# Nine taps in other partitions of a 16-row group, and the first layer's weights in one run per partition

## The chip, the core and the metric

The kernel runs on one core of one Trainium2 chip. The metric is the time of one execution on the device in microseconds (us).

## What is computed

The input `x` has 16 images of 256 channels and 28 x 28 points. It goes through a group normalisation and then through a residual block of two layers, in which each 3 x 3 convolution is replaced by a soft lookup: for every channel the nine values around a point (a patch) are compared with 16 centroids, the softmax over the 16 distances is taken, and it weighs rows of a table made from the centroids and sub-weights. The reference, cut to this:

```python
def amm_conv3x3(x, centroids, w_sub, stride=1):
    B = x.shape[0]
    C, k, s = centroids.shape            # 256, 16, 9
    patches = jax.lax.conv_general_dilated_patches(x, (3, 3), (stride, stride), 'SAME')
    p = patches.reshape(B, C, s, Ho * Wo).transpose(0, 3, 1, 2)
    d = jnp.sum(p * p, axis=-1)[..., None] - 2.0 * jnp.einsum('bncs,cks->bnck', p, centroids) \
        + jnp.sum(centroids * centroids, axis=-1)[None, None]
    attn = jax.nn.softmax(-d, axis=-1)
    lut = jnp.einsum('cks,cso->cko', centroids, w_sub)
    out = jnp.einsum('bnck,cko->bno', attn, lut)
    ...
out = amm_conv3x3(gn(x), centroids1, wsub1)
out = jax.nn.relu(bn_inference(out, bn1_gamma, bn1_beta, bn1_mean, bn1_var))
out = amm_conv3x3(out, centroids2, wsub2)
out = bn_inference(out, bn2_gamma, bn2_beta, bn2_mean, bn2_var)
out = se_layer(out, se_w1, se_b1, se_w2, se_b2)
return x + jax.nn.relu(out + gn(x))
```

## The kernel before

The work is cut into 128 blocks: for each of two layers and 16 images there are four blocks, each one half of the channels (`hh`, 128 of 256) and one half of the rows (`t`, 14 of 28). All is in float32.

**Patches.** The image, normalised and padded to 30 x 30, is written from SBUF to a tensor in HBM, `home1` (layer 1, `to_home1`, L361, with the two halves of image 0's first channel half in two pieces) or `home2` (layer 2, by indirect transfers from POOL, L590). It is written twice for each channel, the second copy one element later, so that two neighbouring taps of one row of the 3 x 3 window are two rows of `home`. The function `patches` (L368 and L372) loads one set into `pt`, a tile of 128 partitions x 8 channel groups x 420. Its 128 partitions are eight groups of 16 rows. Each row of a group is one tap of one channel, or is unused. A set is six transfers: for each line `dy` of the window a large one into 16 partitions (the taps `dx` = 0 and 1, from the two copies) and a small one into 8 partitions (the tap `dx` = 2). Each partition receives eight runs of 418 elements. There are two `pt` tiles, used in turn, and two sets to a block, so 256 sets. A set is issued when PE has finished with the tile that it overwrites. In sets 1 to 4 the small transfers are issued by POOL, in all others by SP.

`tap_row(s)` says into which of the 16 rows tap `s` goes; it is used where the weights for the comparison are laid out on the host and where those of layer 2 are put together on the chip (`prep_wd0`, nine small transfers, far ahead of their use). Row 11 (`BIAS_ROW`) carries a constant. Unused rows hold ones in `pt` and zeros in the weights.

**The rest of a block.** `logits` (L384) multiplies `pt` by the centroids in 32 x 32 tiles; ACT takes the exponential (`exps`, L395); `num_b` and `num_a` (L448, L434) turn it into weighted sums and denominators; DVE takes the reciprocal and spreads it (L476, L491); DVE and POOL scale (`scale_a` L510, `scale_q` L499). `product` (L518) multiplies the results by 128 x 128 weights, seven times for the four blocks of an image in the manner of Strassen, for which POOL forms differences (`mix`, L527) and accumulators are added.

**Weights of the products.** Seven tiles `w_A11` to `w_S4`, of 128 partitions x 9 x 128. For the first layer `load_w` (L194) loads four of them from the input `in_ws1`, of 128 x 18 x 256: nine runs of 128 elements (512 B) for each partition, 1024 B apart. The others are sums and differences of these.

**Order.** It is written out by hand. `at(step, sub, f, ...)` files a call under a step and a place in it; all calls are then made in that order, so that each engine's queue is fixed. Block `j` starts at step `2 j`. The lines that place what the change touches:

```python
at(g + p - NPT, 1.5, patches, u, p, nc.gpsimd if 0 < g + p < 5 else None)
at(1, 1.65, load_w, 0, "A11")
at(3, 1.65, load_w, 0, "S3")
at(3, 1.65, load_w, 0, "A22")
at(6, 0.6, load_w, 0, "A12")
```

SP issues nearly all direct transfers, in this order.

Of the kernel before, what the change touches and what calls it, by code (L numbers as in the profile page):

```python
# [17 lines left out]
P = 128  # L18
# [6 lines left out]
PTW = RT * PW  # L25
K = 16
S = 9
NS = 9
# [26 lines left out]
def digits(h):  # L55
    g, j = h & 7, h >> 3
    return g >> 1, g & 1, j >> 2, j & 3


def tap_row(s):  # L60
    dy, dx = divmod(s, 3)
    return dy + (0, 8, 3)[dx]


BIAS_ROW = 11
# [2 lines left out]
def rows_of(m, c, a):  # L68
    r, c4, mm = c >> 1, 2 * (c & 1) + a, m & 3
    return r, c4, mm, 16 * r + 4 * mm + c4, 16 * (1 - r) + 4 * mm + c4  # L70
# [3 lines left out]
def kernel(  # L74
# [50 lines left out]
    def view(t, off, dims):  # L125
        return bass.AP(t.tensor, t.offset + off, [list(d) for d in dims])
# [62 lines left out]
    def load_w(l, n, eng=None):  # L189
        hh, o = SLOTS[n]  # L190
        t = wl[n]
        eng = eng or nc.sync
        if l == 0:
            eng.dma_start(t, ws1[:, NS * hh : NS * hh + NS, o * P : (o + 1) * P])  # L194
        else:
            eng.dma_start(t[:, 0:8, :], view(d_wa, hh * 8 * P * C + o * P, [[C, P], [P * C, 8], [1, P]]))
            eng.dma_start(t[:, 8, :], d_wb[hh * P : hh * P + P, o * P : (o + 1) * P])
# [165 lines left out]
    def patches(u, p, single=None):  # L363
        hm = (home1 if u["l"] == 0 else home2)[u["b"]]
        at0 = ((u["hh"] * P + 8 * 8 * p) * 2) * HROW + RT * u["t"] * PW
        pt = u["pt", p]
        for dy in range(3):
            nc.sync.dma_start(  # L368
                pt[dy::8, :, : PTW - 2],
                view(hm, at0 + dy * PW, [[HROW, 16], [16 * HROW, 8], [1, PTW - 2]]),  # L370
            )
            (single or nc.sync).dma_start(  # L372
                pt[3 + dy :: 16, :, : PTW - 2],
                view(hm, at0 + dy * PW + 2, [[2 * HROW, 8], [16 * HROW, 8], [1, PTW - 2]]),
            )

# [334 lines left out]
    def prep_wd0():  # L711
        st = stage()
        nc.gpsimd.memset(st[:, :512], 0.0)
        for s in range(S):
            nc.sync.dma_start(
                st[tap_row(s) :: 16, :512].rearrange("p (a k) -> p a k", k=K),
                view(d_sk, s * K, [[S * K, 8], [8 * S * K, 32], [1, K]]),
            )
# [195 lines left out]
    for j, u in enumerate(blocks):  # L914
# [3 lines left out]
        for p in range(2):  # L918
            u["pt", p] = pts[p]
            at(g + p - NPT, 1.5, patches, u, p, nc.gpsimd if 0 < g + p < 5 else None)  # L920
            for q in range(2):
                mm = 2 * p + q
                at(g + p, 0.1 + q, logits, u, mm)
                if wide and mm == 0:
                    at(g, 0.12, wide_copy, u, mm)
                    at(g, 0.9, wide_turn, u, mm)
                    at(g, 1.38, wide_max, u, mm)
                    at(g, 1.39, wide_sub, u, mm)
                    at(g + 1, 1.22, wide_back, u, mm)
                    at(g + 1, 1.89, wide_exp, u, mm)  # L930
                else:
                    at(g + p, 0.12 + q, exps, u, mm)
# [18 lines left out]
    for l in range(2):  # L951
        for b in range(B):
            n = l * B + b
# [48 lines left out]
            else:  # L1002
# [16 lines left out]
                if b == B - 1:  # L1019
                    at(g + 11, 1.9, flags)  # L1020
                    at(g + 12, 2.9, flag_sum)
# [5 lines that stand above are left out]
    for c, sub, m in ((5, 1.96, "S1"), (7, 1.96, "S3"), (7, 2.65, "S2"), (8, 1.96, "S4")):  # L1027
# [80 lines left out]
    with tc.If(rv > 0):  # L1108
        with tc.For_i(0, B, 1) as it:
            t = io.tile([P, NB, HW], F32, tag="xt", name="xt")  # L1110
# [13 lines left out]
            for l in range(2):  # L1124
# [6 lines left out]
                for t2 in range(2):  # L1131
                    us = []
                    for hh in range(2):
                        u = {"l": l, "b": B, "t": t2, "hh": hh, "w": 0, "step": None}
                        for k in range(5):
                            u["qi", k] = hh if k == 4 else 4 * hh + k
                        us.append(u)
                        for mm in range(4):
                            if mm % 2 == 0:
                                u["pt", mm // 2] = pts[mm // 2]  # L1140
                                patches(u, mm // 2)
                            logits(u, mm)
                            wide_copy(u, mm)
                            wide_turn(u, mm)
                            wide_max(u, mm)
                            wide_sub(u, mm)
                            wide_back(u, mm)
                            wide_exp(u, mm)
                        num_b(u)
                        split_r(u)  # L1150
                        join_r(u)
                        split_q(u)
                        join_q(u)
                        recip_dve(u)
                        spread(u, 4)
                        scale_q(u, 4)
                        for mm in range(4):
                            spread(u, mm)
                            num_a(u, mm)
                            scale_a(u, mm)  # L1160
# [23 lines left out]
def _lay_out(inputs):  # L1184

    import numpy as np

    f = lambda n: np.asarray(inputs[n], dtype=np.float32)
    x = f("x")
    bsz, ch = x.shape[:2]  # L1190
    arrays = {"in_x": x.reshape(bsz, ch, -1)}
    cent, wsub = f(_NAMES[0] + "1"), f(_NAMES[1] + "1")
    wd = np.zeros((P, 8, 4, 32), np.float32)
    cwa = np.zeros((P, 8, 4, 32), np.float32)
    cwb = np.zeros((P, 8, 4, 32), np.float32)
    ws = np.zeros((P, NST, ch), np.float32)
    ids = np.zeros((ch, MAPC), np.uint32)
    konst = np.zeros((P, 304), np.float32)
    before = np.zeros((P, 2, ch), np.float32)
    for c0 in range(ch):  # L1200
        i, a, m, c = digits(c0)
        r, c4, mm, rn, rs = rows_of(m, c, a)
        hh = m >> 2
        ka = slice(32 * c + 16 * a, 32 * c + 16 * a + 16)
        for s in range(S):
            wd[32 * i + 16 * a + tap_row(s), m, c, 16 * a : 16 * a + 16] = cent[c0][:, s]
        cwa[ka, m, i, 8 * c4 : 8 * c4 + 8] = cent[c0][:, :8]
        cwb[ka, m, i, rn] = cent[c0][:, 8]
        cwb[ka, m, i, rs] = 1.0
        ws[32 * i + 8 * c4 : 32 * i + 8 * c4 + 8, NS * hh + 2 * mm + r] = wsub[c0, :8]  # L1210
        ws[32 * i + rn, NS * hh + 8] = wsub[c0, 8]
        konst[ka, 3 + c4] = 1.0
        konst[ka, 48 + 32 * mm + rn] = 1.0
        konst[ka, 176 + 32 * mm + rs] = 1.0
        wa = (2 * m + r) * 16 + 4 * i + c4
        ids[c0] = (c0, (2 * c + a) * 32 + 4 * m + i, 2 * wa, 2 * wa + 1, hh * P + 32 * i + rn, 2 * c0, 2 * c0 + 1)
    nhalf = np.zeros((P, P), np.float32)
    for p in range(P):
        konst[p, 0] = p % 32 < 16
        konst[p, 1] = p % 32 >= 16  # L1220
        konst[p, 7 + (p // 16) % 2] = 1.0
        for b in range(2):
            before[p, b, : b * P + p] = 1.0
        nhalf[p, p - p % 16 + BIAS_ROW] = -0.5
        if p % 16 == BIAS_ROW:
            a = (p // 16) % 2
            konst[p, 16 + 16 * a : 32 + 16 * a] = SHIFT / 2
    arrays["in_wd1"] = wd.reshape(P, -1)
    arrays["in_cwa1"] = cwa.reshape(P, -1)
    arrays["in_cwb1"] = cwb.reshape(P, -1)  # L1230
    arrays["in_ws1"] = ws
    cent, wsub = f(_NAMES[0] + "2"), f(_NAMES[1] + "2")
    arrays["in_sk2"] = cent.transpose(0, 2, 1).reshape(ch, -1)
    arrays["in_ks2"] = cent.reshape(ch, -1)
    arrays["in_wsub2"] = wsub.reshape(ch, -1)
    arrays["in_konst"] = konst
    arrays["in_nhalf"] = nhalf
    arrays["in_before"] = before.reshape(P, -1)
    arrays["in_ids"] = ids
    names = [f"L0_conv_bn{l}_{v}" for l in "12" for v in ("gamma", "beta", "mean", "var")] + ["L0_conv_se_b2"]  # L1240
    arrays["in_vec"] = np.stack([f(n).reshape(-1, P).T for n in names], axis=2)
    for n in ("se_w1", "se_b1", "se_w2"):
        arrays["in_" + n] = f("L0_conv_" + n)
    return {n: np.ascontiguousarray(a) for n, a in arrays.items()}, x.shape
# [17 lines left out]
```

## Time and profile before

| | |
|---|---|
| median of 3 runs | 2680.17 us (2678.79 to 2683.46) |
| the profiled execution | 2684.49 us, of which its span is 2683.0 |
| mean granted PE clock in it | 0.993 |
| PE busy / DVE / ACT / POOL | 97% / 66% / 50% / 71% |
| bytes moved by DMA | 374.39 MB, mean 140 GB/s |
| DMA queue of SP (hardware) | 216008 packets, 334.87 MB, 54.0% of 16 engines' span |
| DMA queue of POOL (software) | 6944 packets, 33.95 MB, 3.5% |

The profile is of one execution. PE is the matrix engine, PEld its weight loads, DVE, ACT and POOL the vector, scalar and general engines, SPq the queue of the engine that issues transfers. A row of the timeline gives start, duration, engine, line, operation, output and inputs, and in brackets how long the engine had been idle and what ended that. An `x64` on an `L384` row means 64 matmuls; each float32 matmul of the program stands twice.

### The profile page before, as it was taken

The page shows a single profiled execution, that of the slowest core. Times are in us where ns is not written, and L with a number is a line of the kernel's source. Part 1 is how long each engine was busy: PE and PEld are TensorE (multiplying, and loading weights), DVE is VectorE, ACT ScalarE, POOL GpSimd, SP SyncE. Part 2 cuts the span into 40 slices and gives each one's busy share as a digit, 9 for nine tenths or more (in the row PEclk, how much of TensorE's full clock was granted, in tenths as well). Part 3 has the DMA queues.
Part 4 walks back from the last instruction along what each step waited for, and adds up shares of the span by engine and source line. Part 5 has one row for each costly group of instructions (what it writes and reads, how often), then busy time and mean ns, then how long its engine had stood idle before and what let it go on. Part 6 is the DMA issues. An engine that isn't in the chain of part 4 may idle for free.

```text
span 2683.0 us, 85705 instructions
## 1 busy us (share of the span) xinstructions
PE 2613.8 (97%) x36984; PEld 1261.1 (47%) x36984; DVE 1773.8 (66%) x3786; ACT 1354.7 (50%) x1873; POOL 1903.7 (71%) x1334
## 2 busy tenths in 40 slices
PE   4999999999999999999999999999999999999997
PEld 1344444444444444444444444444444444444444
DVE  4785666667666556656577767677767677767675
ACT  2443444444445444444455555555555655555653
POOL 3755677666776666766578687788787788787786
PEclk8999999999999999999999999999999999999999
DMA  8665667755666666666584555545555555555551
GB/s 180 162 158 147 155 159 201 195 139 138 158 165 168 178 156 145 164 176 158 127 191 108 111 127 123 116 111 109 122 127 123 116 113 108 121 127 123 116 114 51
DMA packets 223337, 374.39 MB, mean 140 GB/s; under 512 B 30360, under 2 KB 193736, under 8 KB 222952
## 3 DMA queue, kind: packets, MB, share of 16 engines
q1 hardware_dynamic: 216008, 334.87, 54.0%
q0 software_dynamic: 6944, 33.95, 3.5%
q8 instruction: 295, 4.83, 0.8%
q14 instruction: 90, 0.74, 0.1%
HBM read 288.93 MB, written 79.80 MB: 137 GB/s over the span
## 4 chain that ended last, share of the span: by engine, by line
PE 86%; DMA 1%; POOL 1%; issue 1%; DVE 1%; ACT 0%; SPq 0%; POOLq 0%; DVEq 0%; ACTq 0%
PE acc L518 46%; PE lg L384 15%; PE na L434 12%; PE nb L448 12%; DMA home<-hpad,col 1%; POOL qp L527 1%; PE sep L814 0%; ACT e L395 0%; DMA pt<-home 0%; PE sep L803 0%; DVE qp L510 0%; DVE rb L491 0%; POOL home L590 0%; POOL qo L525 0%; PE sqp L288 0%
## 5 line engine op out<-in xcount | busy, mean ns | idle before, releaser
L395 ACT ACTIVATE e<-lg 128x784 f32<-128x784 f32 x960 | 738.8, 821 | 720.2 <-PE lg L384 714.9
L527 POOL TENSOR_TENSOR qp<-qp,qp 128x784 f32<-128x784 f32 x512 | 944.6, 1870 | 163.5 <-DVE qp L510 163.0
L518 PE MATMUL acc<-qp,w_S 128*128 128x392 f32 x2048 | 743.2, 503 | 7.7 <-POOL qp L527 6.3
L491 DVE STREAM_SHUFFLE rb<-r 128x392 f32<-128x392 f32 x1024 | 550.6, 604 | 0.0
L518 PE MATMUL acc<-qp,w_A 128*128 128x392 f32 x1536 | 546.5, 499 | 0.1
L518 PEld LDWEIGHTS acc<-qp,w_S 128*128 128x128 f32 x2048 | 376.1, 190 | 356.6 <-POOL qp L527 39.1
L384 PE MATMUL lg<-pt,wd 32*32 32x392 f32 x16384 | 500.6, 504 | 27.0 <-DMA pt<-home 16.3
L518 PEld LDWEIGHTS acc<-qp,w_A 128*128 128x128 f32 x1536 | 284.1, 190 | 247.9 <-DVE qp L510 37.6
L510 DVE TENSOR_TENSOR qp<-na,rb 128x784 f32<-128x784 f32 x352 | 334.1, 972 | 98.1 <-PE na L434 84.9
L462 DVE SCALAR_TENSOR_TENSOR r<-nb,kst,r 128x392 f32<-128x392 f32 x128 | 79.9, 624 | 464.5 <-ACT r L458 464.5
L448 PE MATMUL nb<-e,cwb 64*32 64x392 f32 x8192 | 382.4, 497 | 2.1 <-issue 1.0
L434 PE MATMUL na<-e,cwa 64*32 64x392 f32 x8192 | 377.5, 494 | 0.1
L476 DVE RECIPROCAL r<-r 128x392 f32<-128x392 f32 x128 | 333.2, 2603 | 4.4
L499 POOL TENSOR_TENSOR qp<-qp,rb 128x784 f32<-128x784 f32 x160 | 297.4, 1871 | 2.4
L448 PEld LDWEIGHTS nb<-e,cwb 64*32 64x32 f32 x8192 | 181.4, 107 | 195.8 <-issue 57.1
L384 PEld LDWEIGHTS lg<-pt,wd 32*32 32x32 f32 x16384 | 127.5, 103 | 309.0 <-issue 261.6
L499 POOL TENSOR_TENSOR qo<-qo,rb 128x392 f32<-128x392 f32 x128 | 132.0, 1031 | 197.7 <-DVE rb L487 197.5
L434 PEld LDWEIGHTS na<-e,cwa 64*32 64x32 f32 x8192 | 182.5, 106 | 186.8 <-issue 78.0
L590 POOL DMA_INDIRECT home<-hpad,col x60 | 60.6, 1011 | 185.9 <-DMA home<-hpad,col 91.2
L458 ACT ACTIVATE r<-nb,kst 128x392 f32<-128x392 f32 x128 | 86.8, 678 | 177.4 <-PE nb L448 177.4
L419 POOL TENSOR_TENSOR z<-z,mx 128x1568 f32<-128x1568 f32 x32 | 92.1, 2879 | 86.4 <-DVE mx L413 86.4
L504 ACT COPY qp<-na 128x784 f32<-128x784 f32 x160 | 130.1, 813 | 26.0 <-PE na L434 24.0
(154 smaller groups left out, 1744.5 us busy)
## 6 DMA issues: line engine op xcount, KB each, us to landing
pt<-home SPq DMA_DIRECT2D x768, 209.0 KB
pt<-home SPq DMA_DIRECT2D x756, 104.5 KB
home<-xpad SPq DMA_DIRECT2D x31, 899.0 KB
xt<-in_x SPq DMA_DIRECT2D x30, 784.0 KB
out_dram<-y SPq DMA_DIRECT2D x32, 392.0 KB
w_S<-d_wS SPq DMA_DIRECT2D x4, 576.0 KB
st<-in_wsub SPq DMA_DIRECT2D x4, 512.0 KB
st<-d_wa SPq DMA_DIRECT2D x16, 128.0 KB
```

What stands on the lines that cost most here:

```text
L384: nc.tensor.matmul(bk[32 * c : 32 * c + 32, :N].rearrange("p (r w) -> p r w", w=W), lhsT=wts["wd", u["hh"]][32 * i : 32 * i + 32, mm, c, : ...
L395: nc.scalar.activation(eg[:, 2 * i : 2 * i + 2, :], bk[:, :, :N], AF.Exp, scale=2.0)
L419: nc.gpsimd.tensor_tensor(zk, zk, mx.unsqueeze(2).to_broadcast([P, N // 4, K]), ALU.subtract)
L434: nc.tensor.matmul(bs[32 * i : 32 * i + 32, r, :N], lhsT=wts["cwa", u["hh"]][64 * r : 64 * r + 64, mm, i, :], rhs=es[64 * r : 64 * r + 64, ...
L448: nc.tensor.matmul(bs[32 * i : 32 * i + 32, r, :N], lhsT=wts["cwb", u["hh"]][64 * r : 64 * r + 64, mm, i, :], rhs=es[64 * r : 64 * r + 64, ...
L476: nc.vector.reciprocal(u["r"], u["r"])
L491: nc.vector.stream_shuffle(rb[:, r, :], u["r"], mask_of(2 * mm + r))
L499: nc.gpsimd.tensor_tensor(q, q, u.pop(("rb", mm)), ALU.mult)
L504: nc.scalar.copy(pair(u, mm), u.pop(("na", mm))[:, :, :N])
L510: nc.vector.tensor_mul(pair(u, mm), u.pop(("na", mm))[:, :, :N], rb)
L518: nc.tensor.matmul(accs[key][:, :N], lhsT=wl[w][:, k, :], rhs=us["q", k], start=first and n == 0, stop=last and n == len(ks) - 1,)
L527: nc.gpsimd.tensor_tensor(pair(out_u, mm), pair(in0, mm), pair(in1, mm), ALU.subtract)
```

## The change

The taps of the window go to other rows of the 16-row group. Before, tap (`dy`, `dx`) went to row `dy`, `8 + dy` or `3 + dy` for `dx` = 0, 1, 2. After it a table gives the rows: 0, 8, 5 for `dy` = 0, then 4, 12, 13, then 1, 9, 2. The transfers of a set write to partitions with the same strides (8 for the large one, 16 for the small one) from other starts. Row 11 stays free for the constant.

The input `in_ws1` is laid out on the host as four blocks of 128 rows, each row the 9 x 128 elements of one partition, so that `load_w` reads one run of 4608 B for each partition.

No other instruction is added, removed or moved, on any engine.

```diff
+TAPS = ((0, 8, 5), (4, 12, 13), (1, 9, 2))
+
+
 def tap_row(s):
-    dy, dx = divmod(s, 3)
-    return dy + (0, 8, 3)[dx]
+    return TAPS[s // 3][s % 3]
...
         if l == 0:
-            eng.dma_start(t, ws1[:, NS * hh : NS * hh + NS, o * P : (o + 1) * P])
+            eng.dma_start(t.rearrange("p s n -> p (s n)"), ws1[(2 * hh + o) * P : (2 * hh + o + 1) * P, :])
...
         for dy in range(3):
             nc.sync.dma_start(
-                pt[dy::8, :, : PTW - 2],
+                pt[TAPS[dy][0] :: 8, :, : PTW - 2],
                 view(hm, at0 + dy * PW, [[HROW, 16], [16 * HROW, 8], [1, PTW - 2]]),
             )
             (single or nc.sync).dma_start(
-                pt[3 + dy :: 16, :, : PTW - 2],
+                pt[TAPS[dy][2] :: 16, :, : PTW - 2],
                 view(hm, at0 + dy * PW + 2, [[2 * HROW, 8], [16 * HROW, 8], [1, PTW - 2]]),
             )
...
-    arrays["in_ws1"] = ws
+    arrays["in_ws1"] = ws.reshape(P, 2, NS, 2, ch // 2).transpose(1, 3, 0, 2, 4).reshape(4 * P, -1)
```

## The prediction

> **What bounds the kernel now.** I read the page first: busy time, then the chain that ended last.
>
> ```profile
> span 2683.0 us, 85705 instructions
> PE 2613.8 (97%) x36984; PEld 1261.1 (47%) x36984; DVE 1773.8 (66%) x3786; ACT 1354.7 (50%) x1873; POOL 1903.7 (71%) x1334
> PE 86%; DMA 1%; POOL 1%; issue 1%; DVE 1%; ACT 0%; SPq 0%; POOLq 0%; DVEq 0%; ACTq 0%
> ```
>
> PE runs for 2613.8 of 2683.0 us. All its idle time together is 69.2 us, 2.6% of the span, and nothing that only moves data can win more than this plus what a lowered PE clock costs. So the question is how much of the 69.2 us waits for the two transfers that the diff touches. The view of PE's own waits answers it, first over the whole span (columns: total us, times, longest), then in parts.
>
> ```profile
> PE lg L384 <- DMA pt<-home: 16.3, 4, 8.0
> PE gnp L322 <- DVE gn_mv L317: 13.4, 3, 5.7
> ...
> PE lg L384 <- DMA pt<-home: 11.7, 2, 8.0
> ...
> PE lg L384 <- DMA pt<-home: 3.8, 1, 3.8
> ...
> PE lg L384 <- DMA pt<-home: 0.8, 1, 0.8
> ...
> PE acc L518 <- DMA pt<-home: 0.5, 1, 0.5
> ```
>
> The last four rows are from 0 to 60, 60 to 130, 245 to 600, and 1350 to the end: nearly all of the 16.3 us of waiting for patches lies in the first 104 us, in three waits. The timeline of PE shows them, with the issues on SP's queue that lead to each.
>
> ```profile
> 16.39 0.57 SPq L368 DMA_DIRECT2D pt<-home  x1
> 26.19 4.09 PE L384 MATMUL lg<-pt,wd 32*32 32x392 f32 x64 [8.04 <-DMA pt<-home]
> ...
> 30.38 7.92 SPq L368 DMA_DIRECT2D pt<-home  x6
> 39.94 1.62 PE L384 MATMUL lg<-pt,wd 32*32 32x392 f32 x32 [3.63 <-DMA pt<-home]
> 41.49 5.02 PE L448 MATMUL nb<-e,cwb 64*32 64x392 f32 x64
> ...
> 92.42 0.59 SPq L368 DMA_DIRECT2D pt<-home  x1
> 103.33 1.64 PE L384 MATMUL lg<-pt,wd 32*32 32x392 f32 x32 [3.76 <-DMA pt<-home]
> 104.90 4.03 PE L448 MATMUL nb<-e,cwb 64*32 64x392 f32 x64
> ```
>
> I call these sets A (8.04 us waited), B (3.63) and C (3.76): 15.4 us, all that this change can reach directly. After the fill a set is hidden:
>
> ```profile
> 2003.59 0.54 SPq L368 DMA_DIRECT2D pt<-home  x1
> 2006.60 0.58 SPq L372 DMA_DIRECT2D pt<-home  x1
> ...
> 2020.46 0.94 PE L384 MATMUL lg<-pt,wd 32*32 32x392 f32 x32
> 2005.00:2007.00 2.00, 2.00 (x7) 1.14 (x6) 2.00 (x2) 0.00 (x0) 2.00 (x2) 1.00 0.86 207
> 2009.00:2011.00 2.00, 2.00 (x47) 0.79 (x53) 1.21 (x3) 0.97 (x4) 2.00 (x2) 1.00 0.45 115
> 2011.00:2013.00 2.00, 2.00 (x61) 1.23 (x48) 0.70 (x1) 1.26 (x2) 2.00 (x2) 1.00 0.03 8
> ```
>
> (The last three are windows: length, busy time of PE, PEld, DVE, ACT, POOL, granted clock, DMA share, GB/s.) The set issued from 2003.59 has stopped moving by about 2010.5, since 115 GB/s falls to 8. It is read at 2020.46, so about 10 us of cover is left. If that cover were lost, each further microsecond would be paid in each of 256 sets; nothing in this change comes near 10 us.
>
> **The change, part by part.**
>
> **1. The taps in other rows.** A set is six transfers before and after, in the same order on the same queues (in sets 1 to 4 the three small ones go out on POOL), with the same bytes and run lengths. The issues on SP stay as they are. PE's matmuls read all 32 rows of a block whatever lies in them, so L384 keeps its duration. The weights, the bias row and layer 2's nine small transfers that place weights by tap follow the rows and do not change in number; those nine run some 70 steps before their weights are loaded and cost nothing. What can change is only how fast the six pieces are written, and that matters in A, B and C. The rows for the size and rate:
>
> ```profile
> pt<-home SPq DMA_DIRECT2D x768, 209.0 KB
> pt<-home SPq DMA_DIRECT2D x756, 104.5 KB
> 8.00:10.00 2.00, 0.24 (x1) 0.24 (x2) 1.71 (x2) 0.00 (x0) 1.92 (x2) 1.00 1.06 408
> 14.00:16.00 2.00, 0.00 (x0) 0.00 (x0) 1.93 (x5) 0.00 (x0) 0.00 (x0) 1.00 0.97 207
> 82.00:84.00 2.00, 2.00 (x56) 0.92 (x48) 1.21 (x1) 2.00 (x3) 1.96 (x2) 1.00 0.94 216
> ```
>
> At a DMA share near 1, loads over all 128 partitions move 408 GB/s (8 to 10 us), the half write of the padded image, out of 64 partitions, moves 207 (14 to 16), and patches alone move 216 (82 to 84). Equally busy queues move half as much where a transfer reaches only some of the partitions. So where the pieces go does seem to matter. But the large pieces go to every 8th partition before (rows 0/8, 1/9, 2/10) and after (0/8, 4/12, 1/9): a different start, the same stride, the same 16 partitions apart by 8. One alone should be as slow as before. They go out 1.2 us apart (3.6 us for six), and a large piece of 214,000 bytes takes 214/216 = 1.0 us at the patch rate. Hence neighbouring pieces overlap only in part, and a better spread over the whole set has little to act on.
>
> Bounds for one exposed set. Gain: before, rows 0 to 3 of a 16-row group take four of the nine taps, after it three in any four adjacent rows that start at a multiple of four (3, 2, 2, 2). If such fours were what limits a set, it would take 3/4 of the time: data flow for about 5.5 us (2005 to 2010.5), so 1.4 us sooner. Loss: the small piece to row 5 goes out just ahead of the large one to rows 4/12, the one to row 13 just behind it, in the same fours; if such neighbours slow each other by one large piece's time, a set lands 1.0 us later. I take 0 for each of A, B and C, nearest to the row of one set alone, whose stride stays. Ends: 3 x -1.4 = -4.2 and 3 x +1.0 = +3.0 us.
>
> **2. The weights of the first layer.** Four loads (the second kind of name, `w_S`, is the one at 62.14; a third `w_A` follows it at once), each now one run of 4608 B per partition in place of nine of 512 B:
>
> ```profile
> w_A<-in_ws SPq DMA_DIRECT2D x3, 576.0 KB
> 38.34 1.47 SPq L194 DMA_DIRECT2D w_A<-in_ws  x1
> 62.14 0.45 SPq L194 DMA_DIRECT2D w_S<-in_ws  x1
> 83.91 1.95 SPq L361 DMA_DIRECT2D home<-xpad  x2
> 85.92 1.11 SPq L194 DMA_DIRECT2D w_A<-in_ws  x1
> 85.00:90.00 5.00, 3.57 (x40) 1.35 (x8) 4.43 (x8) 2.61 (x4) 5.00 (x3) 1.00 1.05 333
> 90.00:95.00 5.00, 4.23 (x46) 1.66 (x50) 2.27 (x9) 0.49 (x1) 4.35 (x5) 1.00 0.89 273
> ```
>
> The first three stand before no wait of PE on a DMA: the next such wait after 39.94 is C. The fourth is ahead of C in SP's queue, behind two writes of the padded image (two of 899 KB, 1841 kB). These and the load's 590 kB are 2431 kB; 333 GB/s for 5 us is 1665 kB, and the rest at 273 GB/s takes 2.8 us, so the load ends near 92.8, while C's first piece is only issued at 92.42, after the writes have landed. It is almost out of the way already: I take 0, with -1.1 us as the far end (half of 590 kB at 273 GB/s) and no loss, since the bytes stay.
>
> **3. The clock behind a wait.** After B and C the same work runs slower: L448 takes 5.02 and 4.03 us. Undisturbed rows:
>
> ```profile
> 81.80 2.86 PE L448 MATMUL nb<-e,cwb 64*32 64x392 f32 x64
> 86.81 1.58 PE L518 MATMUL acc<-qp,w_S 128*128 128x392 f32 x4 [1.21 <-POOL qp L527]
> 40.00:42.00 2.00, 2.00 (x40) 0.49 (x48) 0.00 (x0) 0.40 (x1) 0.14 (x1) 0.50 1.09 188
> 88.00:90.00 2.00, 1.78 (x6) 0.68 (x4) 2.00 (x6) 0.00 (x0) 2.00 (x2) 1.00 1.06 374
> ```
>
> Behind the wait of 3.63 us the granted clock is 0.50; behind one of 1.21 it is 1.00. The price is (5.02 - 2.86) + (4.03 - 2.86) for L448 and (1.62 - 0.94) + (1.64 - 0.94) for the L384 before it: 4.7 us. With waits unchanged it is paid as before: 0. If B and C shrink enough it goes too.
>
> [...]
>
> Sum: 0 + 0 + 0, between -4.2 - 1.1 - 4.7 = -10.0 and +3.0. The profiled execution took 2684.49 us (1.5 beyond its span), 4.3 more than the median of 2680.17; the three runs behind the median lie 4.7 apart (2678.79 to 2683.46), so the sum is carried over as it is. A shift of the start moves all that follows by the same amount, PE having no slack behind it. Forecast: 2680 us.
>
> **The rivals.**
>
> *Faster: the spread shortens the sets.* A, B and C land 1.4 us sooner, leaving waits of 6.6, 2.2 and 2.4 us. If 2.2 to 2.4 us is below what lowers the clock, 4.2 + 4.7 = 8.9 us go: 2671.3. If not, 4.2: 2676. For it: patches move at half the rate of 128-partition loads, and the old rows leave 12 to 15 empty. Against it: the stride of 8 stays and the pieces go out 1.2 us apart.
>
> [...]
>
> *Slower: neighbouring pieces collide.* Two pairs in each set (row 5 with rows 4/12, then row 13 with these) are in flight together; at 1.0 us a pair A, B and C land 2.0 us later each, 6 us: 2686.2. It decides only where a set has no cover, and from 10 us later in the steady part. For it: the large pieces already run at half rate. Against it: the old order also sent row 3 between 0/8 and 1/9.
>
> *The change does not act at all* is my forecast in its plainest form, and gives 2680.
>
> **How the numbers follow.** A measurement of this kernel tells about 0.2%, 5.4 us, from no change. Chances: forecast 0.43; sets sooner, clock not relieved (2676) 0.16; sets sooner and clock relieved (2671.3) 0.29; slower rival 0.12. So faster by over 5.4 us 0.29, within 0.59, slower 0.12. The range from 2670 to 2685 holds the first three and leaves out the slower rival; the forecast and the 2676 case alone would span 2675 to 2683, the upper end being +3.0.
>
> **What would show it.** Right: waits of L384 on patches near 8.0, 3.6 and 3.8 us, clock 0.50 behind two of them, PE idle near 69 us, DMA share in the steady windows as before. Faster rival: GB/s well over 216 in windows of patches alone, the waits at 39.94 and 103.33 under 2.5 us, L448 at 2.9 behind them. Slower rival: A's wait over 9 us, fewer than 200 GB/s. The forecast is wrong if PE's idle time moves by over 5 us, above all if it does so after 130 us, where I found nothing that waits for these transfers.

## The result, and the profile after

The changed kernel takes 2672.56 us (median of 8 runs, 2669.08 to 2676.3), the kernel before 2678.88 us (median of 8 runs, 2675.07 to 2683.46). The ratio is 0.9976, with a 95% interval of 0.9965 to 0.9986: 6.3 us or 0.24% faster. The forecast was 2680 within 2670 to 2685. The time lies in the range, but "no change" was wrong, and so was the reason for it.

The page of the kernel after: span, busy times, SP's queue, and the chain that ended last (by engine, then by line). Line numbers are two higher than before.

```profile
span 2671.9 us, 85705 instructions
PE 2606.3 (98%) x36984; PEld 1260.6 (47%) x36984; DVE 1773.1 (66%) x3786; ACT 1353.6 (51%) x1873; POOL 1902.5 (71%) x1334
q1 hardware_dynamic: 211912, 334.87, 51.2%
PE 85%; POOL 2%; DMA 2%; issue 1%; DVE 0%; ACT 0%; SPq 0%; POOLq 0%; ACTq 0%; DVEq 0%
PE acc L520 45%; PE lg L386 15%; PE na L436 12%; PE nb L450 12%; POOL qp L529 2%; DMA home<-hpad,col 2%; POOL qo L527 0%; POOL home L592 0%; ACT e L397 0%; PE sep L816 0%; PE sep L805 0%; DVE qp L512 0%; DMA pt<-home 0%; PE sqp L290 0%; DVE y L857 0%
```

Bytes are the same (334.87 MB), but the queue's transfers keep the 16 DMA engines busy for 51.2% of the span in place of 54.0%. PE's idle time fell by only 3.6 us (69.2 to 65.6); its busy time fell by 7.5 (2613.8 to 2606.3), although it does the same work. So the time that is counted as busy can hold waiting too.

The three exposed sets after, in the timeline of PE:

```profile
26.21 4.09 PE L386 MATMUL lg<-pt,wd 32*32 32x392 f32 x64 [8.10 <-DMA pt<-home]
...
39.09 1.62 PE L386 MATMUL lg<-pt,wd 32*32 32x392 f32 x32 [2.23 <-DMA pt<-home]
40.64 4.99 PE L450 MATMUL nb<-e,cwb 64*32 64x392 f32 x64
...
102.52 1.74 PE L386 MATMUL lg<-pt,wd 32*32 32x392 f32 x32 [3.87 <-DMA pt<-home]
...
1407.82 0.82 PE L520 MATMUL acc<-qp,w_S 128*128 128x392 f32 x2
...
2659.54 0.26 PE L805 MATMUL sep<-ysum,w_sb 128*32 128x1 f32 x4 [1.05 <-DVE fi L887]
```

The last two rows have these partners before, near the end of layer 1 and at the end of the kernel:

```profile
1418.89 0.93 PE L518 MATMUL acc<-qp,w_S 128*128 128x392 f32 x2 [0.54 <-DMA pt<-home]
...
2670.65 0.26 PE L803 MATMUL sep<-ysum,w_sb 128*32 128x1 f32 x4 [1.05 <-DVE fi L885]
```

In this pair sets A and C wait as before; B waits 1.4 us less and starts 0.85 us earlier (39.94 to 39.09), and C starts 0.81 us earlier (103.33 to 102.52). At 1419 the lead is 11.07 us, and at the end it is 11.11.

Two single executions do not place a gain of 6.3 us, though. The spans differ by 11.1, and the profile of the run with the weights alone (below; it has the old rows and no gain) is ahead of the kernel before at the same two rows by 9.78 and 9.70 us (1409.11 and 2660.95). B's shorter wait is no sign of the new rows either: with the old rows in layer 1, it was 2.93 us in the run with the weights alone, 2.45 in the one with new rows in layer 2 only, and 2.69 with the crowded rows. What follows goes by ratios of many runs, and by PE's idle time over the whole of layer 1 (under "Which layer").

One place in layer 1 where this pair's lead grows shows a mechanism. Before (POOL's and PE's timelines):

```profile
492.00 1.07 POOL L590 DMA_INDIRECT home<-hpad,col  x1 [5.77 <-ACT hpad L569]
500.20 0.97 POOL L590 DMA_INDIRECT home<-hpad,col  x1 [7.13 <-DMA home<-hpad,col]
508.65 0.97 POOL L590 DMA_INDIRECT home<-hpad,col  x1 [3.46 <-ACT hpad L549]
...
509.37 1.53 PE L384 MATMUL lg<-pt,wd 32*32 32x392 f32 x32
511.56 1.58 PE L518 MATMUL acc<-qp,w_S 128*128 128x392 f32 x4 [0.66 <-POOL qp L527]
513.36 1.58 PE L518 MATMUL acc<-qp,w_S 128*128 128x392 f32 x4 [0.21 <-POOL qp L527]
515.17 1.58 PE L518 MATMUL acc<-qp,w_S 128*128 128x392 f32 x4 [0.22 <-POOL qp L527]
```

After, the same image:

```profile
487.54 1.07 POOL L592 DMA_INDIRECT home<-hpad,col  x1 [5.78 <-ACT hpad L571]
494.24 0.97 POOL L592 DMA_INDIRECT home<-hpad,col  x1 [5.63 <-DMA home<-hpad,col]
501.47 0.97 POOL L592 DMA_INDIRECT home<-hpad,col  x1 [1.24 <-PE acc L520]
502.47 5.55 POOL L529 TENSOR_TENSOR qp<-qp,qp 128x784 f32<-128x784 f32 x3
...
504.91 0.94 PE L386 MATMUL lg<-pt,wd 32*32 32x392 f32 x32
505.78 4.22 PE L520 MATMUL acc<-qp,w_S 128*128 128x392 f32 x12
```

Layer 1's output goes to `home2` by four scatters that POOL issues, two for each channel half. The second may not be issued before the first has landed, and POOL stands still until then: 7.13 us before, 5.63 here. Behind it in POOL's queue are the differences (`mix`, L527) that PE's next product reads. Before, they come late and PE takes its three groups of four matmuls one by one; after, all twelve run without a gap. The first sign of the stall is in a row that shows no wait: L384 takes 1.53 us in place of 0.94, and this group, which was held up, is recorded as longer, not as idle: one of its matmuls takes 498 ns, those of all L384 rows 504 in the mean.

POOL's wait ahead of this second scatter, in the profiles of the runs below: 8.51 us with crowded rows; 7.13, 7.10 and 6.49 with the old rows in layer 1 (before, layer 2 alone, weights alone); 5.63 and 5.09 with the new ones (after, rows alone); 4.25 with rows 4 to 6. The order with the large pieces first, which has no gain that can be told from none, has 5.23, so a single wait is no measure of the time.

### The profile page after: what moved, and what is told of

It is laid out like the page before. It is cut to its first block, busy times and chain, and to the rows that moved or that the text cites. A ratio compares the mean times of both kernels' runs of the same rounds, so it can differ in the third digit from the quotient of the medians.

```text
span 2671.9 us, 85705 instructions
## 1 busy us (share of the span) xinstructions
PE 2606.3 (98%) x36984; PEld 1260.6 (47%) x36984; DVE 1773.1 (66%) x3786; ACT 1353.6 (51%) x1873; POOL 1902.5 (71%) x1334
## 3 DMA queue, kind: packets, MB, share of 16 engines
q1 hardware_dynamic: 211912, 334.87, 51.2%
## 4 chain that ended last, share of the span: by engine, by line
PE 85%; POOL 2%; DMA 2%; issue 1%; DVE 0%; ACT 0%; SPq 0%; POOLq 0%; ACTq 0%; DVEq 0%
PE acc L520 45%; PE lg L386 15%; PE na L436 12%; PE nb L450 12%; POOL qp L529 2%; DMA home<-hpad,col 2%; POOL qo L527 0%; POOL home L592 0%; ACT e L397 0%; PE sep L816 0%; PE sep L805 0%; DVE qp L512 0%; DMA pt<-home 0%; PE sqp L290 0%; DVE y L857 0%
## 5 line engine op out<-in xcount | busy, mean ns | idle before, releaser
L386 PE MATMUL lg<-pt,wd 32*32 32x392 f32 x16384 | 496.4, 505 | 23.5 <-DMA pt<-home 14.2
L450 PE MATMUL nb<-e,cwb 64*32 64x392 f32 x8192 | 379.3, 499 | 1.4 <-ACT e L397 0.8
L450 PEld LDWEIGHTS nb<-e,cwb 64*32 64x32 f32 x8192 | 180.1, 108 | 193.3 <-issue 51.3
L386 PEld LDWEIGHTS lg<-pt,wd 32*32 32x32 f32 x16384 | 126.3, 103 | 302.8 <-issue 253.7
L592 POOL DMA_INDIRECT home<-hpad,col x60 | 60.4, 1006 | 182.3 <-DMA home<-hpad,col 85.8
```

The costliest lines, as they stand in the source:

```text
L386: nc.tensor.matmul(bk[32 * c : 32 * c + 32, :N].rearrange("p (r w) -> p r w", w=W), lhsT=wts["wd", u["hh"]][32 * i : 32 * i + 32, mm, c, : ...
L450: nc.tensor.matmul(bs[32 * i : 32 * i + 32, r, :N], lhsT=wts["cwb", u["hh"]][64 * r : 64 * r + 64, mm, i, :], rhs=es[64 * r : 64 * r + 64, ...
```

## The experiments

Theories after the result. *Through POOL:* the patch transfers of later sets share the DMA engines with the scatters of layer 1; when they are quicker, the scatters land sooner, POOL's queue moves on sooner, and PE gets its differences in time. *Rival, the fill:* what counts are the exposed sets. *Rival, the weights:* the longer runs do it. And for why the patches are quicker: either the count of taps in four adjacent rows over the whole set, or *neighbours in time*, which means that a piece is slowed by a piece issued next to it into the same four rows.

Each run is compared with runs of the kernel before on the same chip; a ratio has its 95% interval behind it.

### Rows alone, weights alone

The first has the new `TAPS`, `tap_row` and `patches`, with the old `in_ws1`; the second is the reverse.

> The tap rows of the changed kernel with the old layout of the first layer's weights. If the gain comes from the rows (the spread over fours of adjacent partitions), the ratio to before is that of the changed kernel, 0.9976, that is some 6 us faster, the granted DMA share of a steady window falls from about 0.53 to 0.50, and PE's wait at set B is near 2.2 us in place of 3.6. If the gain comes from the weights, the ratio is 1.000 and the wait at B stays 3.6 us.

> The old tap rows with the new layout of the first layer's weights. If the rows are the cause, the ratio to before is 1.000 within 0.1%, with at most 1 us at set C. If the weights are the cause, it is 0.9976. If both add, it is about 0.999.

Rows alone: 0.9977 [0.9965, 0.9989], DMA share of SP's queue 50.8%. Weights alone: 0.9998 [0.9986, 1.0009], 54.0%. All of the gain is the rows'; the weights are worth nothing that can be measured. B's wait was 2.61 us with the rows alone, not 2.2, and 2.93 with the weights alone, not 3.6.

### Other rows

Four more tables, each against the kernel before. The first is the changed kernel with its small pieces exchanged among the same nine rows:

```diff
-TAPS = ((0, 8, 5), (4, 12, 13), (1, 9, 2))
+TAPS = ((0, 8, 2), (4, 12, 5), (1, 9, 13))
```

> The changed kernel with the same nine rows, but the small pieces dealt out otherwise: 2, 5, 13 for the three lines of the window in place of 5, 13, 2. Each four of adjacent rows still takes 3, 2, 2, 2 taps, but no small piece goes out next to a large one in the same four, except row 2 with rows 0/8. If only the count in each four matters, the time equals the changed kernel's (ratio 0.9976). If neighbours in time matter (my slower rival's mechanism), it is faster than the changed kernel by up to 1 us at each of sets A, B and C and by more in the first layer: 0.996 or less.

The second is the kernel before with its small pieces crowded beside the large ones (and the constant in row 15):

```diff
-    return dy + (0, 8, 3)[dx]
+    return (3, 11, 4)[dy] if dx == 2 else dy + 8 * dx
```

> The kernel before with the small pieces in rows 3, 11 and 4 and the constant's row moved from 11 to 15: rows 0 to 3 and 8 to 11 take four taps each, rows 4 to 7 one, rows 12 to 15 none (before: 4, 2, 3, 0). If the fullest four alone sets the time of a set, it equals before (ratio 1.000). If the spread over all the fours matters, it is slower than before by some us: 1.001 to 1.003, with a DMA share above 0.53 in the steady windows. If rows do not matter, 1.000 and a share of 0.53.

The third and fourth put them in rows 4 to 6 and in rows 12 to 14, clear of all large pieces:

```diff
-    return dy + (0, 8, 3)[dx]
+    return dy + (0, 8, 4)[dx]      # third;  (0, 8, 12) in the fourth
...
-                pt[3 + dy :: 16, :, : PTW - 2],
+                pt[4 + dy :: 16, :, : PTW - 2],      # 12 + dy
```

> The kernel before with the small pieces one row further, 4, 5, 6 in place of 3, 4, 5; the large pieces stay at 0/8, 1/9, 2/10. The fours hold 3, 3, 3, 0 taps, and no small piece shares a four with the large piece behind it, but all large ones share the same two fours. If a piece is slowed only by its neighbour in time, this is as fast as the changed kernel or faster: 0.9976 or less, DMA share in the steady windows 0.50 or less. If the large pieces must alternate between fours for a gain, it is close to before: 0.999 to 1.000 and 0.52.

> The kernel before with the small pieces in rows 12 to 14 in place of 3 to 5; the large pieces stay in 0/8, 1/9, 2/10. No small piece lies in the same four rows as the large piece sent next to it. Theory 'neighbours in time': as with rows 4 to 6, 0.992 to 0.994 of the kernel before, DMA share of the whole span 45 to 47%. Rival, that rows 4 to 6 were good for another reason (for being just the fours that the large pieces leave empty, next to row 0 of the same group): 0.997 to 1.000 and 50 to 54%.

And the third again, with the three large pieces of a set issued first and the three small ones after them (a second `for dy in range(3):` ahead of the small ones):

> Rows as in the run with small pieces in 4 to 6, but the three large pieces of a set go out first and the three small ones after them, so that large pieces, which all lie in rows 0 to 3 and 8 to 11, follow each other at once. Theory 'neighbours in time': the share of the DMA engines rises again, to 50% or more, and most of the gain is lost (0.996 to 1.001 of the kernel before). Rival, that what counts is how many of the nine taps lie in four adjacent rows, whatever the order: 45 to 47% and 0.992 to 0.994.

Rows in the order of issue, the ratio, and the share of SP's queue from each page:

| rows in order of issue | median us | ratio | DMA share |
|---|---|---|---|
| 0/8, 3, 1/9, 11, 2/10, 4 | 2685.92 | 1.0046 [1.0029, 1.0062] | 56.6% |
| before: 0/8, 3, 1/9, 4, 2/10, 5 | 2678.88 | 1 | 54.0% |
| 0/8, 1/9, 2/10, 4, 5, 6 | 2674.66 | 0.9991 [0.9978, 1.0004] | 53.4% |
| after: 0/8, 5, 4/12, 13, 1/9, 2 | 2672.56 | 0.9976 [0.9965, 0.9986] | 51.2% |
| 0/8, 2, 4/12, 5, 1/9, 13 | 2662.18 | 0.9955 [0.9938, 0.9972] | 48.2% |
| 0/8, 4, 1/9, 5, 2/10, 6 | 2657.56 | 0.9928 [0.9901, 0.9955] | 45.7% |
| 0/8, 12, 1/9, 13, 2/10, 14 | 2658.10 | 0.9934 [0.9916, 0.9953] | 45.4% |

(The kernel before had medians of 2673 to 2679 us beside these runs; the ratios are what to compare.)

The share and the time come in the same order, but for the last two, whose intervals overlap; the crowded rows cost more than the 1.001 to 1.003 expected. Counting taps in four adjacent rows over the set does not explain it: the table of the change and its exchange have the same nine rows and differ, and rows 4 to 6 have the same rows in both orders of issue, with 45.7% in the one and 53.4% in the other. What fits is neighbours in the order of issue that share four rows (0 to 3, 4 to 7 and so on). With the large pieces in 0/8, 1/9 and 2/10, there are four such pairs at 56.6%, two at 54.0%, and none at 45.7% and 45.4%; the order with the large pieces first has two pairs of large pieces and two of small ones, at 53.4%. With large pieces that take turns between 0/8 and 4/12, there are three at 51.2% and two at 48.2%. For the same number of pairs, taking turns helps too.

The same steady set of layer 2 in windows of 2 us from its first issue shows it for one set. Before, then after, then rows 4 to 6 (length, busy time of PE, PEld, DVE, ACT, POOL, granted clock, DMA share, GB/s):

```profile
2003.59:2005.59 2.00, 2.00 (x7) 1.16 (x7) 2.00 (x8) 1.39 (x2) 2.00 (x2) 1.00 0.28 67
2005.59:2007.59 2.00, 2.00 (x7) 1.14 (x6) 1.58 (x1) 0.33 (x1) 2.00 (x2) 1.00 0.92 181
2007.59:2009.59 2.00, 2.00 (x8) 0.91 (x6) 0.05 (x1) 1.18 (x1) 2.00 (x3) 1.00 0.76 156
2009.59:2011.59 2.00, 2.00 (x58) 1.02 (x66) 1.16 (x3) 1.56 (x5) 2.00 (x2) 1.00 0.30 79
```

```profile
1992.44:1994.44 2.00, 2.00 (x7) 1.16 (x7) 2.00 (x8) 1.39 (x2) 2.00 (x2) 1.00 0.29 78
1994.44:1996.44 2.00, 2.00 (x7) 1.14 (x6) 1.59 (x1) 0.32 (x1) 2.00 (x2) 1.00 0.85 188
1996.44:1998.44 2.00, 2.00 (x8) 0.91 (x6) 0.04 (x1) 1.19 (x1) 2.00 (x3) 1.00 0.71 171
1998.44:2000.44 2.00, 2.00 (x58) 1.03 (x66) 1.16 (x3) 1.56 (x5) 2.00 (x2) 1.00 0.21 45
```

```profile
1988.00:1990.00 2.00, 2.00 (x7) 1.16 (x7) 1.97 (x3) 2.00 (x4) 0.00 (x0) 1.00 0.27 66
1990.00:1992.00 2.00, 2.00 (x7) 1.14 (x6) 2.00 (x3) 1.63 (x2) 0.00 (x0) 1.00 0.84 217
1992.00:1994.00 2.00, 2.00 (x22) 0.91 (x36) 2.00 (x5) 0.00 (x0) 0.82 (x1) 1.00 0.66 167
1994.00:1996.00 2.00, 2.00 (x64) 0.95 (x60) 1.92 (x7) 1.16 (x2) 2.00 (x1) 1.00 0.15 39
```

GB/s times 2 us adds up to about the same bytes (966, 964 and 978 kB). The shares add up to 2.26, 2.06 and 1.92, times 2 us: the 16 engines are busy for 4.5, 4.1 and 3.8 us with one set. PE is busy all the time in all of them.

### Which layer

Rows of the exchange above in layer 2 alone, the old rows in layer 1 (`TAPS[l]`, and `tap_row(s, l)` where weights are laid out):

> The rows of the regrouped kernel (0/8/2, 4/12/5, 1/9/13) in the second layer alone; the first layer keeps the old rows, and the weights of the first layer keep the old layout. Theory: the gain arises where DMA is dense, in the start-up and in the first layer, and the second layer hides every set. Then the ratio to before is 1.000 within 0.1%, while the DMA share of a steady window of layer 2 falls from 0.53 to about 0.46 all the same. Rival: every set costs PE a little wherever it lies; then half of the regrouped kernel's gain appears here, 0.998.

0.9988 [0.9973, 1.0004]: no gain that can be told from none, though the DMA share in layer 2 fell from 0.53 to 0.46. The windows 110 to 1430 (layer 1) and 1500 to 2580 (layer 2) say why. Before, then after (layer 1 alone), then rows 4 to 6:

```profile
110.00:1430.00 1320.00, 1305.41 (x18463) 630.33 (x18462) 846.22 (x1927) 609.27 (x832) 881.82 (x684) 1.00 0.64 160
1500.00:2580.00 1080.00, 1079.95 (x15589) 523.83 (x15590) 764.97 (x1504) 627.48 (x876) 847.59 (x512) 1.00 0.53 117
```

```profile
110.00:1430.00 1320.00, 1307.74 (x18608) 633.61 (x18607) 855.36 (x1944) 613.42 (x839) 891.35 (x690) 0.99 0.62 161
```

```profile
110.00:1430.00 1320.00, 1314.88 (x18769) 640.65 (x18768) 867.05 (x1959) 621.89 (x848) 902.73 (x697) 1.00 0.56 162
1500.00:2580.00 1080.00, 1079.95 (x15526) 524.43 (x15532) 762.63 (x1505) 628.98 (x877) 846.68 (x511) 1.00 0.43 117
```

In layer 2 PE is busy for 1079.95 of 1080 us, with the DMA share at 0.53 and at 0.43 alike: there is nothing to win. In layer 1 PE's idle time goes from 14.6 to 12.3 us with the change and to 5.1 with rows 4 to 6. The same window of the other profiles: 22.7 with crowded rows; 16.1, 15.3 and 14.4 in the runs without a clear gain (layer 2 alone, large pieces first, weights alone); 11.1 with the rows alone, 9.0 with the exchange, 6.6 with rows 12 to 14. This goes with the ratios, and all of it lies behind the exposed sets, the last of which is read at 103 us.

Rows 4 to 6 show that also in aligned rows. Against the run with the weights alone, which took as long as the kernel before, they are 0.49 us behind at the `L448` of set C (104.04 against 103.55), and 16.7 us ahead at the end of layer 1 (weights alone, then rows 4 to 6):

```profile
1409.11 0.93 PE L518 MATMUL acc<-qp,w_S 128*128 128x392 f32 x2 [0.53 <-DMA pt<-home]
...
1392.39 0.82 PE L518 MATMUL acc<-qp,w_S 128*128 128x392 f32 x2
```

### Less to move, and the scatters

The kernel before without the small pieces that SP issues (the taps `dx` = 2 are left out there). These are the small pieces of all sets but the four in which POOL issues them, so the very first set, A, loses them too:

```diff
-            (single or nc.sync).dma_start(
+            if single is not None:
+                single.dma_start(
```

> The kernel before without the small pieces of all sets from the sixth on (the tap dx = 2 is left as it was in the tile; this leaves out a third of the patch bytes). It bounds what lighter DMA can give. If the first layer's PE time depends on how busy the DMA engines are, it is faster than the regrouped kernel: 0.993 to 0.996, nearly all of it before 1430 us. If only start-up counts, sets A and B are untouched by this edit, and the gain is set C's wait, 4 us: 0.9985.

0.9898 [0.9871, 0.9924], DMA share 36.9%: more than either value expected. The expectation that A and B are untouched did not hold for this edit. A's wait fell from 8.04 to 4.03 us, those for patches at B and C were gone, and C's `L448` started at 93.45 us in place of 104.90, so some 10 to 11 us of this gain lie in the fill; in this run's profile PE is idle for 7.6 us in the window of layer 1. The median from issue to landing of the 60 scatters is 5.0 us, against 6.3 before, 5.7 with rows 4 to 6 and 6.8 with the crowded rows (6.2 after the change, 6.4 with the rows alone and with the weights alone, so the median does not tell small changes apart). That fits "through POOL", but less load on the DMA engines could help in other ways, so the next runs touch the scatters.

The kernel before with its four scatters spread out in POOL's queue:

```diff
-at(g + 12 + o + (o and r), (1.95, 1.96)[r] if o == 0 else (1.805, 2.9)[r], to_home2, b, o, r)
+at(*((g + 12, 1.95), (g + 13, 1.805), (g + 13, 2.9), (g + 15, 1.26))[2 * o + r], to_home2, b, o, r)
```

> The kernel before with the four scatters of each first-layer image to home2 placed further apart in POOL's queue, so that POOL does its other work between two scatters and does not stand waiting for the landing of the one before; rows, bytes and transfers are the same. If the first layer loses its time through POOL's wait for scatters that land late, POOL's wait on home falls from 91 us to under 40 and the time falls by 5 to 10 us: 0.996 to 0.998. If POOL's wait has cover and the loss comes some other way (for example PE's own short stalls without a visible releaser), the ratio is 1.000 within 0.1%.

1.0144 [1.0117, 1.0171], slower, where both expectations had it faster or the same. POOL's wait for its own scatters was gone, but PE and ACT had new ones, in the views of their waits (total us, times, longest):

```profile
PE lg L384 <- ACT hpad L549: 26.0, 13, 3.6
ACT hpad L549 <- DMA home<-hpad,col: 133.3, 14, 11.2
```

ACT copies the next image's first sum into `hpad`, and now had to wait until the later scatter had read it. So the run does not decide on the theory. It shows what ties the scatters to their places, and a second way in which a scatter that lands late reaches PE.

So the second scatter of each half was left out, from the second image on, and the shifted copy in `home2` filled with zeros by plain writes on SP's queue, once with the old rows and once with rows 4 to 6:

```diff
-for r in range(2):
-    at(g + 12 + o + (o and r), (1.95, 1.96)[r] if o == 0 else (1.805, 2.9)[r], to_home2, b, o, r)
+at(*((g + 12, 1.95), (g + 13, 1.805))[o], to_home2, b, o, 0)
+at(g + 3, 0.65, zero_u1, b, o)
...
+at(3, 2.9, zeros_make)
```

> The kernel before without the second of the two scatters of each half of layer 1's output, from the second image on: the shifted copy is filled with zeros by plain writes on SP's queue instead, so that the taps of the middle column are left out of layer 2 there, and POOL never waits for a scatter behind another. Theory 'through POOL': what a slow landing costs layer 1 comes by way of POOL's queue, and without that wait the time falls to 2655 to 2664. Rival 'short stalls': PE's stalls in layer 1 come from the busy DMA engines themselves, and the time stays at 2670 to 2679, as the bytes are the same.

> The same as the run without the second scatter, with the small pieces in rows 4 to 6 as well. Theory 'through POOL': without the wait the rows hardly matter, and this lies within 6 us of the run with the old rows. Rival 'short stalls': 15 to 20 us below it, as with the scatters in place.

Old rows: 0.9935 [0.9919, 0.9952], 2658.66 us. Rows 4 to 6: 0.9919 [0.9902, 0.9935], 2654.1 us. The old rows without the second scatter, from their page, move more bytes at a higher share than before:

```profile
span 2659.4 us, 85688 instructions
q1 hardware_dynamic: 220472, 349.14, 56.2%
```

They are still 15.3 us faster than the kernel before beside them (2673.95). So busy DMA engines alone hold PE up little; they do so mostly by way of the scatters. And the other rows, worth 0.72% with the scatters in place, are worth 4.6 us or 0.17% without the second ones (2658.66 - 2654.1), by intervals that overlap. Most of what the rows bring goes through the scatters that POOL waits for.

Three things stay open. This edit takes away POOL's time for issuing 30 scatters (some 30 us over layer 1) along with the wait, so that the two are not told apart. Nor are the two ways from a late scatter to PE: besides POOL's queue there is ACT's copy into `hpad`, which waited for scatters for 48.4 us with the crowded rows, 22.4 with the weights alone, 15.7 before, 18.7 after, and not at all with rows 4 to 6, with rows 12 to 14 or without the second scatters. And the total of POOL's waits for scatters in one profile does not rank small changes: 91.2 us before, 85.8 after, but 81.4 in the run with the weights alone, which had no gain, and 85.9 with the crowded rows, which were slower.

## Why the prediction was right and wrong

**Right.** The weights: 0 expected, 0.9998 measured. PE's durations where nothing holds it up, the queues and set A as stated (8.04 us waited before, 8.10 after). C's wait was 3.76 and is 3.87. B's wait fell by 1.4 us, the size that the bound from fours of adjacent rows gave; that is chance, as runs with the old rows in layer 1 had 2.45 to 2.93 us there.

**Luck: the range.** 2672.56 lies within 2670 to 2685 because the lower end had been drawn to take in the faster rival, and the way of that rival is not the one that the runs show. By the prediction's own yardstick of 5.4 us, the change is faster and not the same.

**Wrong: the step "all that this change can reach directly" are 15.4 us in A, B and C.** That step listed PE's waits for patches and stopped. It did not ask who else uses the DMA engines that the patches keep busy. The chain of waits had the answer: "DMA 1%" of the span was quoted, and its line in the page was not. This is the chain by line, POOL's row in the list of costliest groups, and POOL's waits, before:

```profile
PE acc L518 46%; PE lg L384 15%; PE na L434 12%; PE nb L448 12%; DMA home<-hpad,col 1%; POOL qp L527 1%; PE sep L814 0%; ACT e L395 0%; DMA pt<-home 0%; PE sep L803 0%; DVE qp L510 0%; DVE rb L491 0%; POOL home L590 0%; POOL qo L525 0%; PE sqp L288 0%
...
L590 POOL DMA_INDIRECT home<-hpad,col x60 | 60.6, 1011 | 185.9 <-DMA home<-hpad,col 91.2
...
POOL home L590 <- DMA home<-hpad,col: 91.2, 21, 7.7
```

The transfer on the path to the end is the scatter, not the patch set (`pt<-home` stands at 0%). A steady set had 10 us of cover for itself and gave none to the scatter in flight beside it. The term missing from the sum was about -6 us (2672.56 against 2678.88), put at nothing because no wait for patches was found after 130 us. PE's idle time in layer 1 (14.6 to 12.3 us, and 5.1 with rows 4 to 6) and the aligned rows 4 to 6 show where it arises; how much of the change's own 6 us lies in the fill, one profile cannot say. The share in the chain names the transfer and is no price: after the change it is 2%.

**Wrong: the ceiling of 69.2 us of idle time, and the test "PE's idle time moves by over 5 us".** Idle fell by 3.6 and busy time by 7.5 in this pair (the run with the weights alone, without a gain, has 2605.3 us busy as well, so neither figure prices the change). Held-up groups count as busy (L384 at 509.37), so neither the ceiling nor the test covers all waiting.

**The clock behind B and C: paid as before, as forecast.** Behind B, L386 and L450 take 1.62 and 4.99 us (1.62 and 5.02 before), behind C 1.74 and 3.92 (1.64 and 4.03), so the 4.7 us stayed. The rival had them go if a wait of 2.2 to 2.4 us leaves the clock up. That was the author's estimate, between the 0.50 behind 3.63 us and the 1.00 behind 1.21, and the runs do not show it: with B's wait at 1.86 us (rows 12 to 14) L448 behind it still takes 5.00 us, and 5.09 with a wait of 2.26 (the old rows without the second scatters). The view of groups gives the count, the busy time and the mean ns of one matmul: before behind B (42 to 45 us), after behind B (41 to 44), after undisturbed (80.9 to 83.7), and after ahead of B's wait (33.6 to 36.0).

```profile
L448 PE MATMUL nb<-e,cwb 64*32 64x392 f32 x48 | 4.2, 857 | 0.0
L450 PE MATMUL nb<-e,cwb 64*32 64x392 f32 x48 | 4.2, 857 | 0.0
L450 PE MATMUL nb<-e,cwb 64*32 64x392 f32 x64 | 2.9, 492 | 0.0
L386 PE MATMUL lg<-pt,wd 32*32 32x392 f32 x63 | 3.3, 856 | 0.0
```

A matmul takes 857 ns behind B in both kernels, against 492 undisturbed. After the change it takes 856 ns already ahead of B's wait: PE was as slow before that wait as after it, so a shorter wait could save nothing. The granted clock reads 1.00 there all the same (first row, after); with 857 ns beside it, that reading is not to be trusted here. In the run with the rows alone PE was up to speed when B arrived (L386 took 0.95 us), the wait was 2.61 us, and behind it the clock is 0.50 (second row) and a matmul takes 811 ns:

```profile
40.00:42.00 2.00, 2.00 (x45) 0.57 (x29) 0.00 (x0) 1.25 (x2) 0.56 (x1) 1.00 0.94 237
39.60:42.60 3.00, 3.00 (x48) 1.50 (x39) 0.00 (x0) 1.34 (x2) 0.00 (x0) 0.50 1.06 167
```

With PE up to speed ahead of it, a wait of 2.61 us was followed by 0.50 there; before, the 0.50 was read behind 3.63 us.

**The rivals.** "The spread shortens the sets" gave 2676 or 2671.3 and came near in time. But it went by A, B and C: C's L448 started 0.71 us earlier after the change, and 3.93 with the rows alone, where 1.35 came with the weights alone. And it went by a count over the whole set, which the two orders of rows 4 to 6 refute. "Neighbouring pieces collide" had the right mechanism with the wrong sign here. It counted two pairs in the new order; there are three, as row 2 goes out right behind rows 1/9. The old order held two already (row 3 between 0/8 and 1/9, as the prediction noted), and the new one has large pieces that take turns. Crowding them more, in the run at 1.0046, did cost 0.46%, though not in A, B and C alone.

## What to carry to other kernels

When a change makes a hidden transfer cheaper or dearer, list every transfer that is in flight beside it, and who waits for those: the chain by line names the one that matters. A group that takes longer than its undisturbed like may be a wait, even if no idle time is shown, or a lowered clock: the mean time of one matmul tells which (498 ns in the held-up L384 at 509.37, 857 behind B). And where pieces of a tile are written one after another, it paid here to place each clear of the four rows (0 to 3, 4 to 7 and so on) of the piece issued next to it: rows 4 to 6, the kernel before with one constant changed in two places, gave 0.9928 [0.9901, 0.9955] and beat both kernels of this case.

## What was not expected

The same pieces into the same partitions, issued in another order, change how long the DMA engines are busy: 45.7% against 53.4% of the span. And a load on those engines costs little by itself: at 56.2% the kernel without the second scatters was as fast (0.9935) as one at 45.4% with all of them (0.9934).
